# Counting matrices built by TensorE from one-hots of gathered edge runs, with early products in pieces

## The chip, the cores and the metric

The kernel runs on one core of a Trainium2 chip. The metric is the device time of one execution in microseconds. The engines named are PE (TensorE), DVE (VectorE), ACT (ScalarE), POOL (GpSimd) and SP (SyncE, which here only issues transfers). Each engine works through its own instructions in order and waits at semaphores for the others and for DMA.

## The reference, cut to what matters

A graph network on N = 6250 nodes with 128 features, and E = 106250 edges sorted by destination. Four layers, each with a residual and a layer norm:

```python
x = layernorm(x + sage2(x))    # agg = segment_sum(h[src], dst) / max(deg, 1); agg @ Wl + bl + h @ Wr
                               # twice, with a relu between
x = layernorm(x + gcn64(x))    # (x @ W), norm = dinv[src] * dinv[dst], segment_sum, 128 -> 64 -> 128
x = layernorm(x + gcn2(x))     # two such sums
x = layernorm(x + tag(x))      # three inner layers of three hops:
                               # x = segment_sum(w[:, None] * x[src], dst), w = dinv[src] * edge_weight * dinv[dst]
```

So there are two sums over edges in the first layer, one in the second, two in the third and nine in the last. The first five use the number of edges between two nodes; the nine hops use edge weights.

## The kernel before

**Sums as matrix products.** Nodes are cut into 49 windows of 128. Window s of the sources and a chunk of destination windows make a block of a matrix, 128 sources by up to 512 destinations; an entry of `counts` (one byte) says how many edges go from this source to this destination, an entry of `weights` (f32) their summed weight. The destinations are in 13 chunks: eight of 4 windows, three of 3, two of 4. A sum for a chunk runs over its 49 blocks: `counted_sum` (L479) loads seven blocks of bytes at a time (`columns`, L459 and L462, issued by SP), casts two blocks at a time to f32r (L501, on ACT, or on ACT and DVE by turns), and PE multiplies each block by the source table's high and low half (L508), accumulating in PSUM.

**How the matrices are made.** A setup reads the edges and writes per edge its key (destination and source in one number) to DRAM (`keys`), and rows of 17 edges (`recs`). `counts` and `weights` are zeroed by large DMAs (`empty`). Edges are taken as 49 groups of 128 rows of 17 edges. `cell` (from L660) computes on DVE, for each edge of one group, its address in the matrix (`celli`), how often its key recurs among the 48 following edges (the count, `cval`), and, for the 35 groups that concern the first chunks (`dense`), the summed weight (`wval`). `scatter` (L588) then lets POOL write 128 cells per indirect DMA, 17 DMAs for a group: 833 for the counts, 595 for the weights. POOL's indirect DMAs stand in one line (`in_line`), in the order in which they are written down; the count scatters come first, and the weight scatters follow, spread over the products of later stages by `Paced`.

**The stages.** The first sum (to 1209 us) goes chunk by chunk: fetch the edge groups of the chunk after next, zero another chunk, prepare and scatter the groups of the next chunk, degrees of this chunk (17 one-hots per group at L731 and as many matmuls at L732, `norms`), then the 49 blocks of the first sum. As the second sum's table grows with each finished chunk, the loop also makes a part of the second sum's products: `also` uses the same blocks while they are there (sources of earlier chunks, into `half`), and from the eighth chunk on `early_parts` loads blocks of earlier chunks again, two chunks per turn, 144 blocks in all. The rest of the second sum, 190 blocks, follows (to 1311 us), then the sum of the second layer (to 1533), the two sums of the third layer (tile `cols`, two buffers, to 2180), in which small gathers (`gathered_edges`: tiles `gm`, `ge`) bring rows of edges for the hops, standing in POOL's line behind the weight scatters; DVE unpacks them at L882 to L896. The nine hops, which load `weights` (L1245) and gather rows for the remaining destinations, last to the end.

The loads of the first sum use the seven parts of one large room in turn (`slots`).

Of the kernel before, what the change touches and what calls it, by code (L numbers as in the profile page):

```python
# [47 lines left out]
P = 128  # L48
# [39 lines left out]

SLOTS, LOADS, STEP, HOTS, GROUP = 30, 12, 2, 5, 4
# [18 lines left out]
def width(c):  # L108
    return len(windows_of(c)) * P
# [27 lines left out]
def load_weights(nc, a, const, work, ps, ident, tags):  # L137
# [18 lines left out]
    transposed("w1l", a["L0_gnn_W1l"])  # L156
    transposed("w1r", a["L0_gnn_W1r"])
    transposed("w2l", a["L0_gnn_W2l"])
    transposed("w2r", a["L0_gnn_W2r"])
    bcast("b1l", a["L0_gnn_b1l"], D)  # L160
    bcast("b2l", a["L0_gnn_b2l"], D)
# [22 lines left out]
def kernel(ctx: ExitStack, tc: tile.TileContext, a: dict, out: bass.AP):  # L184
# [15 lines left out]
    counts = dram.tile([BASE[NC] + 4 * NB * KD * P, 1], U8, name="counts")  # L200
# [6 lines left out]
    def empty(mats, dt, c, engine):  # L207
        n = 7 * width(c) // (4 if dt == U8 else 16)
        z = zeros[:].bitcast(dt)[:, :n]
        ins = fills[dt, c] = engine.dma_start(  # L210
            mats[BASE[c]:BASE[c + 1]].rearrange("(p s f) o -> p s (f o)", p=P, f=n),
            z.unsqueeze(1).to_broadcast([P, NW * width(c) // n, n])).ins
        tc.declare_no_dep(ins, group=f"cells {dt}", reason="another chunk")
        tc.add_to_no_dep_group(f"cells {dt}", ins)
        return ins

    with tc.tile_pool(name="setup", bufs=1) as setup, \
            tc.tile_pool(name="ps_setup", bufs=2, space=PSUM) as ps:

        def spread(name, ap, dt):  # L220
            t = setup.tile([P, L + 2 * J], dt, name=name)
            nc.sync.dma_start(t[:], bass.AP(ap.tensor, ap.offset, [[L, P], [1, L + 2 * J]]))
            return t
# [4 lines left out]
        dsti = spread("dsti", a["dst"], I32)  # L228
# [3 lines left out]
        main = slice(J, J + L)  # L232


# [3 lines left out]
        nc.vector.tensor_scalar(k1[:], dsti[:], 1023, 13, op0=ALU.bitwise_and, op1=ALU.logical_shift_left)  # L238
        nc.vector.tensor_scalar(k2[:], dsti[:], 20, 23, op0=ALU.logical_shift_right, op1=ALU.logical_shift_left)
# [5 lines left out]
        nc.sync.dma_start(keys[J:].rearrange("(p e) o -> p (e o)", p=P), key[:, main])  # L245


        def field(at):
# [18 lines left out]
        empty(counts, U8, 0, nc.sync)  # L267

# [7 lines left out]
        dst = setup.tile([P, L + 2 * J], F32, name="dst")  # L276
# [6 lines left out]
        nc.vector.tensor_sub(t1[:], dst[:, 2 * J:2 * J + L], dst[:, main])  # L283
        nc.vector.tensor_scalar(t2[:], dst[:, main], float(NOWHERE), None, op0=ALU.is_lt)
        nc.vector.scalar_tensor_tensor(t2[:], t1[:], 0.0, t2[:], op0=ALU.is_equal, op1=ALU.mult)
        nc.vector.tensor_reduce(odd[:, 1:2], t2[:], AX.X, ALU.max)
        nc.vector.tensor_scalar(t2[:], t1[:], float(NOWHERE // 2), None, op0=ALU.is_lt)
        nc.vector.scalar_tensor_tensor(t2[:], t1[:], 1024.0, t2[:], op0=ALU.is_ge, op1=ALU.mult)
        nc.vector.tensor_reduce(odd[:, 2:3], t2[:], AX.X, ALU.max)
# [3 lines left out]
        dmax = setup.tile([P, RPP], F32, name="dmax")  # L293
        nc.vector.tensor_reduce(dmin[:], by_row(dst[:, main]), AX.X, ALU.min)
        nc.vector.tensor_reduce(dmax[:], by_row(dst[:, main]), AX.X, ALU.max)
        rowi = setup.tile([P, RPP], I32, name="rowi")
        nc.gpsimd.iota(rowi[:], pattern=[[1, RPP]], base=0, channel_multiplier=RPP)
        nc.vector.tensor_scalar(rowi[:], rowi[:], ~(P - 1), None, op0=ALU.bitwise_and)
        even = setup.tile([P, RPP], F32, name="even")
        nc.vector.tensor_copy(even[:], rowi[:])  # L300
        d1 = setup.tile([P, RPP], F32, name="d1")
        d2 = setup.tile([P, RPP], F32, name="d2")
        nc.vector.tensor_sub(d1[:], dmax[:], even[:])
        nc.vector.tensor_scalar(d1[:], d1[:], float(2 * P), None, op0=ALU.is_ge)
# [3 lines left out]
        nc.vector.tensor_sub(d2[:], dmin[:], even[:])  # L308
        nc.vector.tensor_scalar(d2[:], d2[:], -float(P), None, op0=ALU.is_lt)
# [6 lines left out]
        row = setup.tile([P, RPP], F32, name="row")  # L316
        nc.gpsimd.iota(row[:], pattern=[[1, RPP]], base=1, channel_multiplier=RPP,
                       allow_small_or_imprecise_dtypes=True)
# [43 lines left out]
    with tc.If(go == 1) as fork:  # L362
        usual_way(tc, a, out, dram, ident, part, first, over, keys, recs, edges, counts, weights, fills, empty)
# [5 lines left out]
def usual_way(ctx, tc, a, out, dram, ident, part, first, over, keys, recs, edges, counts, weights, fills, empty):  # L369
# [9 lines left out]
    iota = const.tile([P, NEAR * P], F16, name="iota")  # L379
    nc.gpsimd.iota(iota[:], pattern=[[1, NEAR * P]], base=0, channel_multiplier=0,  # L380
# [12 lines left out]
    stacked = early.tile([P, DH], F32, name="stacked")  # L393
    nc.vector.tensor_add(stacked[:], ident[:, :DH], ident[:, DH:])
    wt = load_weights(nc, a, early, work, ps, ident, ("y", "pp"))
# [63 lines left out]
    def columns(t, c, mat, dt, step, s0, ws=None):  # L459
        cw, s1 = width(c), min(s0 + step, NW)  # L460
        if ws is None:
            load = nc.sync.dma_start(t[:, :(s1 - s0) * cw], mat[BASE[c]:BASE[c + 1]].rearrange(  # L462
                "(p f) o -> p (f o)", p=P)[:, s0 * cw:s1 * cw]).ins
        else:
            n = len(ws) * P
            load = nc.sync.dma_start(
                t[:, :(s1 - s0) * n].rearrange("p (s f) -> p s f", f=n),
                mat[BASE[c]:BASE[c + 1]].rearrange("(p s f) o -> p s (f o)", p=P, f=cw)[:, s0:s1, :n]).ins
        needs = [ins for i in blocks_of(ws or windows_of(c)) for ins in scattered[dt, i]]
        tc.declare_no_dep(load, group=f"cells {dt}", keep=needs, reason="others' cells")  # L470
        tc.add_to_no_dep_group(f"cells {dt}", load)
        for ins in needs:
            tc.add_manual_dep(load, ins.name, SYNC, reason="the matrix is complete")
        return t
# [4 lines left out]
    def counted_sum(pool, c, parts, turns, own=False, wide_bufs=3, slots=None, since=0, until=NW, also=None):  # L479
# [5 lines left out]
        for s in range(since, until):  # L485
            r = (s - since) % step
            if r == 0:
                t = next(slots) if slots is not None else pool.tile([P, step * CW], U8, name="cols", tag="cols")
                t = columns(t, c, counts, U8, min(step, until - s), s)
                if own:  # L490
                    for j, w in enumerate(windows_of(c)):
                        if s <= w < min(s + step, until):
                            loop = t[:, (w - s) * cw + j * P:(w - s) * cw + (j + 1) * P]
                            nc.vector.tensor_tensor(loop, loop, ident8[:], op=ALU.add)
            if not todo:
# [5 lines left out]
                copy(wide[:, :n * cw], t[:, r * cw:(r + n) * cw])  # L501
                todo = [wide[:, i * cw:(i + 1) * cw] for i in range(n)]
            cols = todo.pop(0)
            for into, of_block, begin, end in [(acc, parts, since, until)] + ([also] if also else []):
                if s < end:
                    lhss = of_block(s)
                    for i, lhs in enumerate(lhss):
                        product = nc.tensor.matmul(into[:, :cw], lhs, cols, start=s == begin and i == 0,  # L508
                                                   stop=s == end - 1 and i == len(lhss) - 1).ins
                paced.product(product, len(lhss))  # L510
# [16 lines left out]
    kept = ctx.enter_context(tc.tile_pool(name="kept", bufs=1))  # L527
# [18 lines left out]
    KNOWN, AHEAD = START[ND], 8  # L546
    halves = {c: dram.tile([P, width(c)], F32, name=f"half{c}") for c in range(1, NC)}
    early_parts = {c: dram.tile([P, width(c)], F32, name=f"early{c}") for c in range(AHEAD)}
# [32 lines left out]
    def scatter(mat, dt, vals, i):  # L581

        group = f"cells {dt}"
        needs = [fills[dt, c] for c in chunks_near(i) if (dt, c) in fills]
        mine = scattered[dt, i] = []
        bounds = {} if dt == U8 else {"bounds_check": mat.shape[0] - 1, "oob_is_err": False}
        for k in range(KD):
            ins = nc.gpsimd.indirect_dma_start(  # L588
                out=mat[:], out_offset=bass.IndirectOffsetOnAxis(ap=celli[:, i, k:k + 1], axis=0),
                in_=vals[:, i, k:k + 1], in_offset=None, **bounds).ins  # L590
            tc.declare_no_dep(ins, group=group, keep=needs, reason="no cell is written twice")
            tc.add_to_no_dep_group(group, ins)
            for need in needs:
                tc.add_manual_dep(ins, need.name, SYNC, reason="empty")
            if dt == F32:
                tc.add_manual_dep(ins, last_count.name, ORDER, reason="needed later")
            mine.append(in_line(ins))
            yield ins
        queue.append(mine[-1])

    class Paced:

        PRODUCTS, GROUP, FIRST = 3.4, 8, 80

        def __init__(self, todo):
            self.todo, self.products, self.begun = todo, 0, 0
            self.some(self.FIRST)

        def some(self, n, behind=None):
            for i in range(n):  # L610
                ins = next(self.todo, None) if self.todo else None
                if ins is not None and i == 0 and behind is not None:
                    tc.add_manual_dep(ins, behind.name, SYNC, reason="the products go ahead")

        def product(self, ins, n):
            self.products += n
# [1001 lines left out]
```

## Time and profile before

| | |
|---|---|
| Time, median of 3 runs | 5791.16 us (5787.49 to 5791.88) |
| Profiled execution | 5791.37 us |
| Its span | 5789.5 us |
| Mean granted TensorE clock | 0.969 |
| PE busy | 5254.7 us (91%) |
| POOL busy | 4158.4 us (72%) |
| DVE busy | 3115.3 us (54%) |
| ACT busy | 2141.4 us (37%) |

The stages, from the table of stretches of the trace (length, busy time of PE, PEld, DVE, ACT and POOL with the number of instructions, granted clock, DMA share, GB/s):

```profile
0.00:33.60 33.60, 1.04 (x3) 0.63 (x3) 27.38 (x53) 7.87 (x7) 1.38 (x11) 1.00 0.69 242
33.60:163.00 129.40, 1.84 (x4) 0.73 (x4) 75.85 (x271) 8.11 (x19) 91.60 (x93) 1.00 0.51 151
163.00:1209.00 1046.00, 757.18 (x3534) 525.63 (x3535) 552.83 (x2123) 439.45 (x586) 800.30 (x807) 0.86 0.63 193
1311.00:1533.00 222.00, 205.03 (x988) 156.37 (x987) 202.54 (x536) 166.36 (x249) 179.73 (x139) 0.98 0.62 179
1533.00:2180.00 647.00, 619.04 (x2925) 512.13 (x2924) 394.31 (x897) 314.79 (x436) 391.57 (x356) 0.99 0.48 137
2180.00:5789.50 3609.50, 3572.44 (x11538) 1868.49 (x11538) 1787.68 (x4748) 1156.77 (x3062) 2614.12 (x2727) 0.99 0.93 316
```

A stage is read by comparing the busy times with its length: the engine whose time comes near to the length bounds it. DMA-issuing work isn't counted as busy on SP, and POOL's busy time here is its indirect DMAs being issued. PEld is the loading of weights for PE and runs beside it. Busy time is less than the time a queue is taken where an engine pauses between instructions, which the groups list as idle time "<-issue".

### The profile page before, as it was taken

To read this page: it belongs to the slowest core of one execution; us is meant where nothing else is said; L and a number is where in the kernel's file an instruction comes from. 1 tells how busy PE (TensorE), PEld (TensorE's weight loads), DVE (VectorE), ACT (ScalarE), POOL (GpSimd) and SP (SyncE) were. 2 spreads that over 40 slices of the span, in tenths; PEclk is the share of its full clock that TensorE was granted. 3 is DMA by queue.
4 is the path that set the end of the run, shared out by engine and by line. 5 is a ranking of instruction groups with operands and counts; after the bars stand their busy time and mean duration, and the time that the engine had idled before them with its cause. 6 is when DMAs were issued, how large, how long until landed. Compare 5 with 4: busy or idle time off the path is not lost.

```text
span 5789.5 us, 70572 instructions
## 1 busy us (share of the span) xinstructions
PE 5254.7 (91%) x19487; PEld 3143.9 (54%) x19487; DVE 3115.3 (54%) x8828; ACT 2141.4 (37%) x4433; POOL 4158.4 (72%) x4204
## 2 busy tenths in 40 slices
PE   0656579799999899999999999999999999999998
PEld 0334457576788784555555555555555555555455
DVE  7685455258855564444446554444456544444566
ACT  1323346347755442323333323323333333233332
POOL 5777777778877617767767767767777677777775
PEclk9878789899999999999999999999999999999999
DMA  5768785146544449999999999999999999999997
GB/s 184 237 201 248 217 260 154 59 140 177 155 131 137 129 139 333 323 319 325 324 318 310 309 313 323 322 321 323 323 302 312 301 326 324 316 323 324 304 336 264
DMA packets 707889, 1517.46 MB, mean 262 GB/s; under 512 B 153094, under 2 KB 359962, under 8 KB 707226
## 3 DMA queue, kind: packets, MB, share of 16 engines
q1 hardware_dynamic: 524642, 1272.39, 65.1%
q0 software_dynamic: 134080, 180.02, 11.5%
q10 hardware_dynamic: 48760, 60.45, 3.1%
q8 instruction: 155, 2.54, 0.2%
q14 instruction: 252, 2.06, 0.1%
HBM read 1313.22 MB, written 199.20 MB: 261 GB/s over the span
## 4 chain that ended last, share of the span: by engine, by line
PE 71%; DMA 11%; POOL 7%; DVE 6%; issue 4%; ACT 1%; ACTq 0%; SPq 0%; POOLq 0%; DVEq 0%
PE acc L1245 45%; PE acc L508 14%; DMA rows<-stored,gsrc 7%; PE gacc L1212 5%; POOL counts L588 5%; PE pp L435 3%; PE pd L732 1%; DMA cols<-counts 1%; POOL weights L588 1%; PE half L508 1%; DMA slots<-counts 1%; DVE widev L501 1%; DMA counts<-cval,celli 1%; ACT wides L501 1%; POOL rows L1148 1%
## 5 line engine op out<-in xcount | busy, mean ns | idle before, releaser
L1245 PE MATMUL acc<-weighed,hop 128*128 128x512 f32 (+1 forms) x7154 | 3402.6, 591 | 13.2 <-DMA weighed<-weights 6.8
L1148 POOL DMA_INDIRECT rows<-stored,gsrc x2727 | 2614.1, 959 | 981.9 <-issue 347.5
L1195 ACT ACTIVATE both<-rows,gwgt 128x128 fp32r<-128x128 f32 x2718 | 1047.8, 400 | 1969.7 <-DMA rows<-stored,gsrc 1783.5
L1212 PE MATMUL gacc<-both,oh 128*128 128x256 f32 x2718 | 1761.2, 657 | 7.9 <-DVE both L1196 7.9
L1245 PEld LDWEIGHTS acc<-weighed,hop 128*128 128x128 f32 x7154 | 1169.7, 190 | 941.2 <-issue 837.6
L1196 DVE SCALAR_TENSOR_TENSOR both<-rows,gwgt,both 128x128 fp32r<-128x128 f32 x2718 | 923.8, 350 | 1334.1 <-ACT both L1195 1323.6
L508 PE MATMUL acc<-wides,t 128*128 128x512 f32 (+1 forms) x3083 | 875.7, 394 | 359.2 <-ACT wides L501 240.3
L588 POOL DMA_INDIRECT counts<-cval,celli x833 | 828.6, 995 | 263.0 <-issue 245.1
L1212 PEld LDWEIGHTS gacc<-both,oh 128*128 128x128 f32 x2718 | 514.6, 190 | 651.8 <-issue 396.2
L508 PEld LDWEIGHTS acc<-wides,t 128*128 128x128 f32 x3083 | 569.8, 191 | 496.9 <-ACT wides L501 267.1
L588 POOL DMA_INDIRECT weights<-wval,celli x595 | 677.2, 1138 | 181.4 <-issue 167.1
L501 ACT CAST wides<-slots 128x1024 fp32r<-128x1024 uint8 (+3 forms) x684 | 562.3, 862 | 521.5 <-DMA slots<-counts 309.2
L508 PE MATMUL acc<-widev,t 128*128 128x512 f32 (+1 forms) x2044 | 576.8, 390 | 31.5 <-DVE widev L501 27.0
L1175 DVE TENSOR_TENSOR oh<-places,gdst 128x640 fp32r<-128x640 f32 x604 | 473.3, 784 | 213.1 <-PE gacc L1212 212.2
L508 PEld LDWEIGHTS acc<-widev,t 128*128 128x128 f32 x2044 | 376.8, 190 | 112.9 <-DVE widev L501 42.8
L731 DVE TENSOR_SCALAR oh<-iota,dloc 128x384 bf16<-128x384 f16 x833 | 214.2, 320 | 366.8 <-PE pd L732 366.7
L501 ACT CAST wides<-cols 128x1024 fp32r<-128x1024 uint8 (+1 forms) x364 | 285.0, 797 | 298.5 <-DMA cols<-counts 160.7
L501 DVE CAST widev<-cols 128x1024 fp32r<-128x1024 uint8 (+1 forms) x364 | 249.8, 691 | 175.2 <-PE acc L508 137.5
L508 PE MATMUL half<-wides,t 128*128 128x512 f32 (+1 forms) x606 | 188.6, 390 | 0.0
L732 PE MATMUL pd<-oh,lw 128*4 128x384 bf16 x833 | 175.4, 334 | 10.1 <-DVE oh L731 8.1
L501 DVE CAST widev<-slots 128x1024 fp32r<-128x1024 uint8 (+3 forms) x239 | 155.8, 669 | 18.2 <-PE acc L508 13.0
L1065 DVE TENSOR_TENSOR y<-pp,dinvw 128x256 f32<-128x256 f32 (+2 forms) x153 | 82.4, 539 | 139.0 <-PE pp L435 138.7
(266 smaller groups left out, 2790.4 us busy)
## 6 DMA issues: line engine op xcount, KB each, us to landing
weighed<-weights SPq DMA_DIRECT2D x1728, 512.0 KB
weights<-zeros SPq DMA_DIRECT2D x8, 12544.0 KB
slots<-counts SPq DMA_DIRECT2D x174, 448.0 KB
cols<-counts SPq DMA_DIRECT2D x140, 448.0 KB
rows<-stored,gsrc POOLq DMA_INDIRECT x2727
counts<-zeros SPq DMA_DIRECT2D x10, 3136.0 KB
weighed<-weights SPq DMA_DIRECT2D x96, 256.0 KB
stored<-hop ACTq DMA_DIRECT2D x74, 256.0 KB
```

Source lines behind the costliest of these rows:

```text
L435: nc.tensor.matmul(pm[:, j * d:(j + 1) * d], xt[:, j * P:(j + 1) * P], w, start=True, stop=True)
L501: copy(wide[:, :n * cw], t[:, r * cw:(r + n) * cw])
L508: product = nc.tensor.matmul(into[:, :cw], lhs, cols, start=s == begin and i == 0, stop=s == end - 1 and i == len(lhss) - 1).ins
L588: ins = nc.gpsimd.indirect_dma_start(out=mat[:], out_offset=bass.IndirectOffsetOnAxis(ap=celli[:, i, k:k + 1], axis=0), in_=vals[:, i, k:k ...
L731: nc.vector.tensor_scalar(oh[:], iota[:], dloc[:, k:k + 1], None, op0=ALU.is_equal)
L732: nc.tensor.matmul(acc[:], lw[:, k, :], oh[:], start=k == 0, stop=k == KD - 1)
L1148: nc.gpsimd.indirect_dma_start(out=fetched_rows[:, self.slot(self.asked), :], out_offset=None, in_=stored[self.h % 2][:], in_offset=bass.I ...
L1175: nc.vector.tensor_tensor(oh[:, :m, :], places[:].unsqueeze(1).to_broadcast([P, m, P]), gdst[:, i, ks].unsqueeze(2).to_broadcast([P, m, P] ...
L1195: nc.scalar.activation(both[:, :D], x, AF.Copy, scale=w)
L1196: nc.vector.scalar_tensor_tensor(both[:, D:], x, w, both[:, :D].bitcast(F32), op0=ALU.mult, op1=ALU.subtract)
L1212: nc.tensor.matmul(self.acc[:, j * 2 * D:(j + 1) * 2 * D], oh, both, start=k == 0, stop=k == KG - 1)
L1245: nc.tensor.matmul(acc[:, :cw], tables[h][:, s, :], t[:, s % STEP * cw:(s % STEP + 1) * cw], start=s == 0, stop=s == NW - 1)
```

## The change

**Counts.** `counts` is one DRAM tile per chunk now, laid out window by window, and no longer zeroed or scattered to. The setup also writes `runs`, 128 keys and 128 weights from each row of 17 edges on, and `begin`, the row from which the edges of four neighbouring nodes are sure to be found. POOL gathers one run for every four nodes (128 runs, that is four windows, in one indirect DMA; 13 of them). `prepared` splits the keys of a batch into zone (source window and which of the four nodes) and place (source within its window), transposes them, and takes the degrees from the same run. For 8 groups of four nodes `hot` makes a zone one-hot (8 x 196) and a place one-hot (8 x 128) on DVE; one matmul per group multiplies them, which gives the counts of four destinations from all sources, and ACT writes two groups at a time as bytes into the window's tile `built`, in runs of eight bytes. SP stores a finished window. Loads read a chunk's seven blocks as one run of 896 bytes per window and partition; casts read them across the windows.

**Pace.** `Meanwhile` is called after every block and does a share of a generator: of the building, 64 evictions in 49 blocks, 81 having been done before the first; and of the zero fills of `weights`, cut into 63 pieces of 1.84 MB, all of which SP issues.

**Weights.** The cells of three edge groups and their 51 scatters come behind each chunk of the first sum, in POOL's one line with the gathers of the runs. The pacing of the weight scatters over later stages is gone.

**Early products.** They begin with the fourth chunk and come in pieces of seven blocks, five pieces a turn (two in the last but one), always for the chunk with most to do: 294 blocks in place of 144, so that 40 remain. The room for loads has five parts, the wide tiles of the first sum two buffers for three, and most of the weights are loaded after the first sum.

```diff
+    def building():
+        found, spots = {}, {}
+        found[0] = gathered_run(0)
+        for w in range(NW):
+            b, c = w // WPB, chunk_of(w)
+            if w % WPB == 0:
+                if b + 1 < NBATCH:
+                    found[b + 1] = gathered_run(b + 1)
+                spots[b] = prepared(b, found.pop(b))
+            t = spare if w % 2 else cells.tile([P, NW * P], U8, name="built")[:]
+            by_column = t.rearrange("p (s f) -> p s f", f=P)
+            for some in range(GROUPS_W // SOME):
+                k0 = w % WPB * GROUPS_W + some * SOME
+                zone = hot("zone", zones2, spots[b], k0, NZ)
+                place = hot("place", places2, spots[b], P + k0, P)
+                for pair in range(SOME // 2):
+                    acc = ps_build.tile([P, 2, CW // 2], F32, name="some")
+                    for i in range(2):
+                        nc.tensor.matmul(acc[:, i, :NZ], place[:, pair, :, i], zone[:, pair, :, i],
+                                         start=True, stop=True)
+                    f = some * SOME * G + pair * 2 * G
+                    nc.scalar.copy(by_column[:, :, f:f + 2 * G].rearrange("p s (i d) -> p s i d", d=G),
+                                   acc[:, :, :NZ].rearrange("p i (s d) -> p s i d", d=G))
+                    yield
+            nc.sync.dma_start(counts[c].rearrange("(w p f) o -> w p (f o)", w=SHAPE[c], p=P)[w - START[c]], t)
+    def hot(name, places, spots, k0, n):
+        t = hots.tile([P, SOME // 2, n, 2], BF16, name=name)
+        nc.vector.tensor_tensor(
+            t[:], places[:].unsqueeze(1).to_broadcast([P, SOME // 2, n, 2]),
+            spots[:, k0:k0 + SOME].rearrange("p (j o) -> p j o", o=2).unsqueeze(2).to_broadcast(
+                [P, SOME // 2, n, 2]), op=ALU.is_equal)
+        return t
+    def gathered_run(b):
+        t = cells.tile([P, 2 * RUN], F32, name="run", bufs=3)
+        ins = nc.gpsimd.indirect_dma_start(
+            out=t[:], out_offset=None, in_=runs[:],
+            in_offset=bass.IndirectOffsetOnAxis(ap=begin[:, b:b + 1], axis=0)).ins
+        queue.append(in_line(ins))
+        return t
...
+    meanwhile = Meanwhile()
+    meanwhile.add(building(), 4 * PAIRS_W / NW)
+    meanwhile.some(0, 5 * PAIRS_W + 1)
...
+    meanwhile.add(filling, (ND + 1) * FILLS / (NW * 11))
...
     for c in range(NC):
-            fetch_chunk(c + 2)
-            if c + 4 < NC:
-                empty(counts, U8, c + 4, nc.sync)
-            count_cells(c + 1)
-            for i in sorted(i for i in blocks_near(c) if i in degs):
-                degrees(i)
-            norms(c)
...
-            for e in range(2 * (c - ND + 1), 2 * (c - ND + 2)):
-                if 0 <= e < AHEAD:
-                    half = fetched_sums(halves[e]) if e > 0 else None
-                    acc = counted_sum(counted, e, both(t1hi, t1lo), [(2, "s")], slots=slots,
-                                      since=START[e], until=KNOWN)
+            for e, since, m in pieces.get(c, ()):
+                half = fetched_sums(partial[e]) if e in partial else None
+                acc = counted_sum(counted, e, both(t1hi, t1lo), [(2, "s")], wide_bufs=2, slots=slots,
+                                  since=since, until=since + m, meanwhile=meanwhile)
...
+            for i in dense[PER * c:PER * (c + 1)]:
+                filled(chunks_near(i))
+                cell(i, fetch(i))
+        meanwhile.rest()
-    last_count = queue[-1]
-    paced = Paced(ins for i in dense for ins in scatter(weights, F32, wval, i))
...
-                copy(wide[:, :n * cw], t[:, r * cw:(r + n) * cw])
+                copy(wide[:, :n * cw].rearrange("p (s w f) -> p s w f", s=n, f=P),
+                     t[:, :, r:r + n, :].rearrange("p w s f -> p s w f"))
```

## The prediction

> **What bounds the kernel now.** I read the stretches of the span first, then the groups, then the waits up to 1209 us, where the last product of the first sum ends.
>
> ```profile
> 300.00:400.00 100.00, 68.75 (x314) 39.67 (x315) 74.34 (x286) 31.57 (x44) 77.44 (x75) 0.85 0.72 222
> 1000.00:1100.00 100.00, 72.45 (x376) 57.32 (x375) 26.00 (x106) 40.13 (x58) 76.23 (x79) 0.86 0.18 55
> 1209.00:1311.00 102.00, 98.10 (x500) 79.96 (x499) 74.70 (x204) 48.02 (x76) 79.66 (x73) 0.95 0.58 168
> 1430.00:1530.00 100.00, 93.75 (x466) 73.14 (x466) 95.47 (x247) 80.72 (x126) 81.92 (x60) 1.00 0.66 187
> 1600.00:1700.00 100.00, 99.41 (x440) 79.61 (x439) 56.53 (x95) 51.63 (x67) 78.06 (x73) 1.00 0.47 135
> 2500.00:2600.00 100.00, 99.35 (x311) 50.47 (x310) 38.22 (x94) 26.53 (x71) 60.53 (x64) 1.00 0.93 314
> ```
>
> The columns are length, busy us of PE, PEld, DVE, ACT and POOL, the granted clock, the DMA share and GB/s. Until 1209 no engine is full: PE has 50 to 95 us in 100 and POOL stands at 76 throughout. That is an issuing queue: 79 scatters in 100 us, 1.27 us each. From 1209 (rest of the second sum) to 2180 PE is the bound, except in the next layer's sum (1311 to 1533), where DVE has 95. The hops from 2180 on are full on PE and DMA; the diff leaves them alone.
>
> ```profile
> L588 POOL DMA_INDIRECT counts<-cval,celli x833 | 828.6, 995 | 263.0 <-issue 245.1
> L588 POOL DMA_INDIRECT weights<-wval,celli x595 | 677.2, 1138 | 181.4 <-issue 167.1
> L501 ACT CAST wides<-slots 128x1024 fp32r<-128x1024 uint8 (+3 forms) x684 | 562.3, 862 | 521.5 <-DMA slots<-counts 309.2
> L508 PE MATMUL acc<-widev,t 128*128 128x512 f32 (+1 forms) x2044 | 576.8, 390 | 31.5 <-DVE widev L501 27.0
> L731 DVE TENSOR_SCALAR oh<-iota,dloc 128x384 bf16<-128x384 f16 x833 | 214.2, 320 | 366.8 <-PE pd L732 366.7
> ```
>
> The count scatters, 833 x 1.27 = 1058 us, pace the first sum: its loads of counts wait for them, which the waits show (total us, times, longest).
>
> ```profile
> ACT wides L501 <- DMA slots<-counts: 309.2, 11, 90.8
> PE acc L508 <- DMA slots<-counts: 123.1, 2, 118.7
> ```
>
> **The change, by steps.** Base: the profiled execution, 5791.37 us (span 5789.5 and 1.9 around it); the three runs have a median of 5791.16, the same thing.
>
> *Removed:* 833 count scatters, the counts' zero fills, and 833 one-hots and matmuls for degrees. *Added on DVE:* 196 zone and 196 place one-hots (1568 and 1024 bf16) and 13 preparations of a gathered run; *on PE* 1568 matmuls of 196 columns; *on ACT* 784 evictions of 392 elements; *on SP* 49 stores of 802 KB. One zone with its place is a "hot" and makes 4 evictions. Hots are spread so that one falls to 3.06 blocks (81 evictions go ahead, then 64 in 49 blocks).
>
> ACT per hot: the PSUM copy of 384 columns takes 0.477, so 0.483 for 392, x4 = 1.93, and casts of 3.06 blocks at 1.045 a pair 1.60: 3.5 us. An eviction writes bytes in runs of 8; the nearest strided row is the edge copy with 4-byte elements 12 bytes apart (L270, 850 elements 1.354 against 0.907 for L264): ends 0.48 and 0.70; I take 0.48, since 8 bytes lie together. In "SBUF — State Buffer", Specifications, the Trainium skill asks for two hits per 16-byte line; eight-byte runs would meet that, the edge copy, one or two per line, would not, and its row agrees; by the rule the sum stays, by the row it gains 784 x 0.22, at most 172 us on ACT.
>
> DVE per hot: 2592 elements. Two-operand rows run at one element a tick (816 elements 0.995, 512 0.685, so 1.02 ns each): 2.8 us. The only row with all operands 16 bits wide, L731, takes 0.257 us for 384 back to back, 0.67 ns each: 1.7 us; I take 1.7, since that row is nearest in type, and keep 2.8. The rule in "VectorE: DVE Perf Modes", Mode 2x_1P, gives a two-tensor operation two elements per cycle where all are 16-bit with unit step; the 816-element rows have f32 inputs and can't show it; by the rule a hot is about 1.5 and the sum stays, by the f32 rows it is rival (b), 100 us more. Besides hots, a chunk carries 3 cell preparations (about 7 us each: four operations of 816 elements and some 17 of 0.17), one run's preparation (about 7) and the stage's work (about 8): 36 us. Over 16 hots (chunks 0 to 2) that makes 3.95 a hot, over 27 (chunks 3 to 7, with early pieces) 3.0, less than ACT's 3.5.
>
> PE per hot: 8 matmuls between 0.094 (half of L732's 384 columns, 0.184) and 0.184, and 3.06 blocks of two or four products at 0.234: 2.3 to 4.4; I take 2.9 in most segments.
>
> So without further waits: first products at about 118 us (163 now): 64 evictions of 0.5 from about 70, then a store and a load of about 12; chunks 0 to 2 at 16 x 3.95 + 11 = 74 each (11 being the turn of a chunk: L563 waits up to 11.0 us); chunks 3 to 7 at 27.4 x 3.55 + 11 = 108; chunks 8 to 12, the build over, 290 together (for chunk 8: 162 products of 384 columns at 0.175, 70 of 512 at 0.234, turn 11). 118 + 222 + 540 + 290 = 1170, 39 less than now.
>
> *After the first sum.* 40 blocks remain of 190: 40 x 2 x 0.234 = 19 on PE, and about 6 us of stage work per chunk now rules: 77 for 102, so -25. POOL's weight scatters have then been done, and with them goes this stall near 1991:
>
> ```profile
> 1985.85 0.24 DVE L882 TENSOR_SCALAR gdst<-gm 128x17 f32<-128x17 f32 x1 [11.42 <-DMA gm<-recs,gat]
> ...
> 1991.78 2.07 PE L508 MATMUL acc<-widev,t 128*128 128x512 f32 x4 [14.68 <-DVE widev L501]
> ```
>
> The gathers stood behind POOL's scatters, DVE stood in them, and PE lost 15: -16 with its tail. Counts are loaded in 896-byte runs for 3584 and cast from a strided view. I cost both at nothing from 1311 on: DMA share 0.47 to 0.66 covers the loads; if 20% slower (262 GB/s at share 0.95 while fills ran, 868 to 903, against 314 in the hops), loads of 3.5 us pass the 3.3 in which PE uses one, and 140 of them lose up to 0.6 each, 84. If the DVE cast of 1024 (0.69) falls to one element a tick (1.1), the 239 of the sum at 95% lose about 100.
>
> *What is moved, and the step that decides.* The 595 weight scatters move into the first sum, 51 behind each chunk's three cells. POOL issues in order, and the gathers of the runs stand in the same line: in the changed order of POOL, the gathers for batches 4, 5, 6, 7, 9, 10 and 12 each come directly behind 51 scatters: 51 x 1.27 = 65 us, 69 with the landing. In DVE's order the preparation that waits for the gather comes only 8 to 12 hots after the first of these cells' indices (from hot 29 to 41, 49 to 57, 64 to 73, 92 to 100, 112 to 120, 134 to 143, 158 to 167). At 3.5 to 4 us that is 28 to 48 us: DVE arrives first and waits. Behind the waiting preparation stand all later hots, hence matmuls, evictions, SP's store and the count loads behind the store. As a cycle: 69 us from a cell to its preparation, then the hots to the next cell at 3.5 to 3.9: 100 + 96 + 141 + 112 + 118 + 122 + 176 = 865 us from hot 29 (13 behind the 16 sent ahead, about 150) to the last (1015). Add 20 to the end of chunk 7 and 290: 1325, 116 later than 1209. The weights' fills (63 of 1.84 MB on SP, two to four pressed in front of the first chunks' cells) could hold a scatter for the 7 us that one takes at 262 GB/s; within the range.
>
> Sum: 5791 + 116 - 25 - 16 = 5866 us.
>
> **Rivals.** (a) *The gathers are in time:* DVE arrives later than I count, or POOL issues faster without count work. For it: 36 us of DVE per chunk may fall between cell and preparation; against: the positions in order. Then 1170 stands: 5791 - 39 - 25 - 16 = 5711, faster. It decides once the first sum ends by 1250 (1209 + 25 + 16), that is, once the seven waits cost it under 80 us, 11 each. (b) *Hots at one element a tick:* 2.8 for 1.7. The cycle then has 104 hots outside its waits at about 4.3 for 3.7, 62, and the 29 before it are 1.1 longer each, 32: with chunk ends about +100, 5966. For it: every two-operand row; against: none of those has 16-bit inputs. (c) *Eviction at 0.70, or slow casts or loads later on:* ACT to 4.4 a hot adds 50 to 80; casts or loads up to 100: 5920 to 5965. (d) *The transfers fill up:* fills, stores and loads of chunks 3 to 7, some 32 MB in 108 us, 296 GB/s, against 262 to 314 seen at full share; if they set the pace with neither waits nor gains, 5780 to 5800.
>
> **How the numbers follow.** Forecast 5866 with its own range 5820 to 5910: chance 0.45; (a) 0.17; (b) 0.13; (c) 0.17; (d) 0.08. (a) reaches down to 5711 with part-waits above it, so the range starts at 5730 and leaves about one in ten out below; above, 5985 takes in (b) and (c) one at a time and leaves both at once out. A measurement can tell 0.2% here, 11.6 us. Faster: (a) and a third of (d), 0.20; same: 0.05; slower: 0.75.
>
> **What would show it.** DVE waiting for the DMA of a run, seven times of 20 to 40 us, before 1020, with POOL in scatters of weights meanwhile: right. No such wait and a first sum ending near 1170: rival (a). A zone one-hot of 1.6 us rather than about 1.05: (b). An eviction mean over 0.6, a DVE cast over 0.9: (c). DMA share over 0.9 with loads as the longest wait: (d). PE's 15 us gap before the last sum's end should be gone and the hops last 3608 as now; if the hops change, the sum is wrong in a place I did not look.

## The result, and the profile after

The changed kernel takes 5842.4 us (median of 4 runs, 5837.23 to 5845.64) against 5790.8 for the kernel before: 1.0089 times as long, 95% interval 1.0072 to 1.0107. Its profiled execution took 5844.81 us, span 5842.9, clock 0.967. The forecast was 5866, and the mechanism that it called likeliest was the right one.

Stages are told by the same events in both traces: the last product with `w2r` ends the first sum, the last with `wconv` the rest of the second, the last with `wlin` the second layer's sum, the first with `weighed` the third layer. The prediction's 1209, 1311 and 1533 us were read from other events, so only differences of lengths are held against it.

| stage ends at, us (length) | before | after | difference of lengths |
|---|---|---|---|
| first sum | 1214.7 | 1318.2 | +103.5 |
| rest of the second sum | 1357.5 (142.8) | 1450.8 (132.6) | -10.2 |
| second layer | 1543.5 (186.0) | 1632.3 (181.5) | -4.5 |
| third layer | 2173.5 (630.0) | 2227.4 (595.1) | -34.9 |
| hops, last such product | 5773.9 (3600.4) | 5827.5 (3600.1) | -0.3 |

The sum of the differences is 53.6 us; the profiled executions differ by 53.4.

The waits of the changed kernel up to 1400 us (total us, times, longest):

```profile
DVE ki L778 <- DMA run<-runs,begin: 298.2, 8, 46.4
PEld L866 <- DVE place L830: 255.2, 19, 45.0
PE some L866 <- DVE place L830: 248.7, 14, 44.7
POOL weights L648 <- DVE low L755: 182.5, 4, 64.4
```

DVE waits for gathered runs, and PE behind it for the next one-hots. Of the eight waits for runs one, of 4.9 us, is for the very first run. Now DVE's timeline, the first instruction of each preparation (start, duration; in brackets the wait before it):

```profile
172.82 0.21 DVE L778 CAST ki<-run 128x128 int32<-128x128 f32 x1
229.56 0.23 DVE L778 CAST ki<-run 128x128 int32<-128x128 f32 x1 [35.82 <-DMA run<-runs,begin]
334.75 0.23 DVE L778 CAST ki<-run 128x128 int32<-128x128 f32 x1 [40.70 <-DMA run<-runs,begin]
434.07 0.23 DVE L778 CAST ki<-run 128x128 int32<-128x128 f32 x1 [39.46 <-DMA run<-runs,begin]
572.70 0.23 DVE L778 CAST ki<-run 128x128 int32<-128x128 f32 x1 [46.35 <-DMA run<-runs,begin]
575.96 0.22 DVE L778 CAST ki<-run 128x128 int32<-128x128 f32 x1
686.97 0.23 DVE L778 CAST ki<-run 128x128 int32<-128x128 f32 x1 [43.23 <-DMA run<-runs,begin]
814.35 0.23 DVE L778 CAST ki<-run 128x128 int32<-128x128 f32 x1 [44.59 <-DMA run<-runs,begin]
816.25 0.22 DVE L778 CAST ki<-run 128x128 int32<-128x128 f32 x1
943.94 0.23 DVE L778 CAST ki<-run 128x128 int32<-128x128 f32 x1 [43.15 <-DMA run<-runs,begin]
```

Seven waits of 36 to 46 us stand before batches 4, 5, 6, 7, 9, 10 and 12, while 8 and 11, whose gathers were issued right behind the ones before, have none. POOL's timeline gives the other half of the first one: a scatter of the first cells at 152.02, the gather behind the 51 of them at 226.76. The other bursts of 51 in front of a gather take as long, 71.6 to 75.1 us from the first scatter to the gather.

```profile
152.02 1.03 POOL L648 DMA_INDIRECT weights<-wval,celli  x1 [86.63 <-DVE celli L756]
...
226.76 0.99 POOL L766 DMA_INDIRECT run<-runs,begin  x1 [0.30 <-issue]
```

In the stretches of 200 us no engine of the changed kernel is full in the first sum (the columns are as before):

```profile
118.00:318.00 200.00, 125.24 (x659) 81.28 (x657) 120.50 (x259) 125.61 (x236) 107.72 (x93) 0.84 0.74 224
318.00:518.00 200.00, 125.46 (x679) 80.79 (x680) 117.97 (x242) 127.85 (x241) 90.14 (x76) 0.83 0.67 209
518.00:718.00 200.00, 106.27 (x562) 68.44 (x561) 87.15 (x183) 103.93 (x194) 98.77 (x94) 0.77 0.60 182
```

The later stages, in the same columns (the end of the first sum, then about the second layer, the third and the hops), are as full as they were:

```profile
1030.00:1318.00 288.00, 249.85 (x1209) 198.46 (x1208) 88.96 (x255) 176.36 (x241) 221.56 (x213) 0.98 0.43 117
1401.00:1625.00 224.00, 203.84 (x975) 156.35 (x975) 199.29 (x538) 165.01 (x250) 0.00 (x0) 0.97 0.61 167
1625.00:2233.00 608.00, 597.44 (x2913) 507.90 (x2912) 377.64 (x890) 318.04 (x433) 33.07 (x30) 1.00 0.52 145
2233.00:5842.90 3609.90, 3569.32 (x11542) 1864.93 (x11541) 1793.27 (x4748) 1162.00 (x3062) 2616.02 (x2727) 0.99 0.93 317
```

And the groups that answer to those of before:

```profile
L648 POOL DMA_INDIRECT weights<-wval,celli x595 | 670.9, 1128 | 565.3 <-DVE low L755 182.5
L544 ACT CAST wides<-slots 128x1024 fp32r<-128x1024 uint8 (+3 forms) x703 | 611.8, 885 | 226.0 <-PE half L552 83.5
L552 PE MATMUL acc<-widev,t 128*128 128x512 f32 (+1 forms) x1964 | 538.8, 386 | 24.9 <-DVE agg L564 12.7
```

The count scatters are gone, and with them the 309 us in which ACT waited for counts; from 1401 us on POOL issues nothing until the next small gathers for the hops. In the first sum, up to 718 us, PE, DVE and ACT are each busy 44 to 64% of the time, and the transfers are at 0.60 to 0.74: a picture of engines that wait for one another in turn.

### The profile page after: what moved, and what is told of

Same layout as the page of the kernel before. It is cut to its first block, busy times and chain, and to the rows that moved or that the text cites. A ratio compares the mean times of both kernels' runs of the same rounds, so it can differ in the third digit from the quotient of the medians.

```text
span 5842.9 us, 70969 instructions
## 1 busy us (share of the span) xinstructions
PE 5292.9 (91%) x20205; PEld 3176.3 (54%) x20205; DVE 3119.8 (53%) x7885; ACT 2464.2 (42%) x5187; POOL 3345.4 (57%) x3393
## 5 line engine op out<-in xcount | busy, mean ns | idle before, releaser
L552 PE MATMUL acc<-wides,t 128*128 128x512 f32 (+1 forms) x3163 | 993.9, 409 | 77.6 <-ACT wides L544 69.5
L544 ACT CAST wides<-slots 128x1024 fp32r<-128x1024 uint8 (+3 forms) x703 | 611.8, 885 | 226.0 <-PE half L552 83.5
L552 PE MATMUL acc<-widev,t 128*128 128x512 f32 (+1 forms) x1964 | 538.8, 386 | 24.9 <-DVE agg L564 12.7
L866 PE MATMUL some<-zone,place 128*128 128x196 bf16 x1568 | 265.4, 267 | 271.2 <-DVE place L830 248.7
L1004 POOL DMA_INDIRECT gm<-recs,gat x17 | 18.0, 1059 | 849.3 <-DVE gwgt L1021 846.7
L544 ACT CAST wides<-cols 128x512 fp32r<-128x512 uint8 (+1 forms) x364 | 289.1, 798 | 238.2 <-PE acc L552 182.2
L866 PEld LDWEIGHTS <-place 128*128 128x128 bf16 x1568 | 118.8, 103 | 419.1 <-DVE place L830 255.2
L869 ACT CAST slots<-some 128x392 uint8<-128x392 f32 x384 | 177.1, 513 | 151.7 <-PE some L866 143.2
L869 ACT CAST built<-some 128x392 uint8<-128x392 f32 x400 | 184.6, 516 | 133.5 <-PE some L866 130.1
L830 DVE TENSOR_TENSOR zone<-zones,spots 128x1568 bf16<-128x1568 bf16 x196 | 189.9, 969 | 73.8 <-PE some L866 73.3
```

The source lines that it names most:

```text
L544: copy(wide[:, :n * cw].rearrange("p (s w f) -> p s w f", s=n, f=P), t[:, :, r:r + n, :].rearrange("p w s f -> p s w f"))
L830: nc.vector.tensor_tensor(t[:], places[:].unsqueeze(1).to_broadcast([P, SOME // 2, n, 2]), spots[:, k0:k0 + SOME].rearrange("p (j o) -> p ...
L866: nc.tensor.matmul(acc[:, i, :NZ], place[:, pair, :, i], zone[:, pair, :, i], start=True, stop=True)
L869: nc.scalar.copy(by_column[:, :, f:f + 2 * G].rearrange("p s (i d) -> p s i d", d=G), acc[:, :, :NZ].rearrange("p i (s d) -> p s i d", d=G))
```

## The experiments

**Gathers asked for earlier.**

```diff
-            t = cells.tile([P, 2 * RUN], F32, name="run", bufs=3)
+            t = cells.tile([P, 2 * RUN], F32, name="run", bufs=6)
-            found[0] = gathered_run(0)
+            found.update((b, gathered_run(b)) for b in range(4))
-                    if b + 1 < NBATCH:
-                        found[b + 1] = gathered_run(b + 1)
+                    if b + 4 < NBATCH:
+                        found[b + 4] = gathered_run(b + 4)
```

> Edit: the gathers of the runs are asked for four batches ahead instead of one (six run buffers for three); nothing else moves. Theory (the line on POOL decides): DVE's wait for the runs, 298.2 us in 8 times in the changed kernel, falls under 30, POOL's scatters stay at 595, and the first sum ends at about 1180 instead of 1318 (the no-wait sum of the prediction was 1170); time about 5705. Rival (the waits hide work that would set the pace anyway, ACT at 3.5 us a hot, the turns of the chunks, transfers): the waits go but the first sum ends at 1250 or later, time 5775 or more.

**Weights scattered later.** `scatter` becomes a generator again and is paced by `Paced`, as in the kernel before.

```diff
             nc.vector.tensor_add(wval[:, i, :], w, f1[:])
-            scatter(i)
...
         meanwhile.rest()
+    paced = Paced(ins for i in dense for ins in scatter(i))
```

> Edit: the cells are still prepared in the first sum, but the 595 scatters of weights are issued after it, paced over later products as before the change; the gathers of the runs stay one batch ahead. Theory (the line): without scatters in front of them the gathers come in time, the first sum ends near 1180 as with gathers asked for earlier. The later stages get back what the scatters cost there: the gap of 15 us on PE near the end of the third layer and, if the rest of that layer's 35 us less came from POOL's scatters too, all 35: about 5740. Rival for the 35 (the new layout of the counts or its loads brought 20 of them): only 15 return, about 5720. Rival for the first sum (other work sets the pace): 5790 or more.

**Early products as before the change.**

```diff
-        for c in PIECES:
-            known, pieces[c] = START[c + 1], []
...
+        for c in range(ND - 1, NC):
+            for e in range(2 * (c - ND + 1), 2 * (c - ND + 2)):
+                if e < ND:
+                    pieces.setdefault(c, []).append((e, START[e], START[ND] - START[e]))
+                    done[e] = START[ND]
```

> Edit: the second sum's early products as before the change (144 blocks, two chunks a turn from the eighth chunk on), everything else as changed, so 192 blocks remain instead of 126. Theory (POOL's line sets the pace of a chunk, 51 scatters each): without pieces a chunk of the build has 16 hots and still 69 us of scatters in front of the next gather, so the waits grow in number, to 10 or more and over 350 us; the first sum gets longer, about 1390, and the rest of the second sum 10 longer: about 5920. Rival (pieces only add products to the first sum): it gets 66 x 2 x 0.234 = 31 us shorter, time about 5825.

These three fell on a chip where the kernel before took 7821.74 us. They gave 6899.82, 6808.57 and 6924.71 there; none of the expectations in microseconds can be held against that. Their traces did show the mechanism: no wait for a run, but for the first of about 5 us, with gathers asked for earlier or weights scattered later, and 296.0 us of them in 9 times with the early products of before. All three were run again, beside a fourth, on a chip where the kernel before takes 5801.74.

> The kernel of e1_runs_ahead again (runs asked for four batches ahead, scatters of weights where the change put them), because its first runs fell on a chip where the kernel before took 7821.74 us instead of 5791. Theory (POOL's line): no wait of DVE for a run; with the build then bound at about 3.57 us a hot, as the weights-late kernel showed from 75 to 775 us, the first sum ends between 1050 and 1120; time 5600 to 5680. Rival (the scatters themselves, sharing the transfers with fills, stores and loads, hold the loads back): the waits for runs go but loads of counts take their place; first sum at 1200 or later, 5730 or more.

Measured: 5588.08 us (5580.08 to 5591.78), ratio to the kernel before 0.9631 (0.9615 to 0.9647). The first sum ends at 1055.2 instead of 1318.2. DVE's timeline has no wait at the same instructions, except the very first of 4.89 us. Four of the thirteen:

```profile
197.20 0.32 DVE L778 CAST ki<-run 128x128 int32<-128x128 f32 x1
258.35 0.32 DVE L778 CAST ki<-run 128x128 int32<-128x128 f32 x1
326.01 0.22 DVE L778 CAST ki<-run 128x128 int32<-128x128 f32 x1
404.65 0.21 DVE L778 CAST ki<-run 128x128 int32<-128x128 f32 x1
```

And the stretches show what the waits had held back, on every engine:

```profile
118.00:318.00 200.00, 170.47 (x909) 109.92 (x908) 169.45 (x367) 171.77 (x323) 135.64 (x101) 0.96 0.95 293
318.00:518.00 200.00, 175.52 (x975) 112.23 (x973) 150.87 (x313) 179.78 (x339) 161.15 (x128) 0.98 1.02 313
518.00:718.00 200.00, 166.95 (x889) 109.83 (x887) 147.05 (x308) 159.93 (x300) 160.46 (x130) 0.94 0.95 284
```

The same 595 scatters are still issued beside the first sum, from 151.7 to 1059.6 us. So it was the place of the gathers in POOL's line, not the scatters' work, that made the change slower: moving 13 gathers takes 263 us out of the first sum. The rival's sign is missing too: between 118 and 790 us ACT waits only 5.6 us for loads of counts.

> The kernel of e2_weights_late again (scatters of weights after the first sum, paced over later products). Theory: first sum at about 1040 as in its first run, the rest of the third layer back to about 630 from 595, the rest of the second sum and the second layer's sum a little longer with scatters beside them (by up to 15): about 5620. Rival (the scatters' cost comes back in full where they stand now, since POOL still needs 595 x 1.27 = 756 us before the hops' gathers): the hops start late, 5750 or more.

Measured: 5567.93 us (5566.14 to 5574.56), ratio 0.9594 (0.9577 to 0.961). First sum 1038.7, rest of the second 131.3, second layer 185.2, third layer 594.5, hops 3607.2. The rival fell. The first sum and the total were as expected or better, but the return to 630 in the third layer did not come, although POOL is full of scatters there:

```profile
1355.00:1455.00 100.00, 100.00 (x458) 82.81 (x458) 61.50 (x113) 54.73 (x70) 78.78 (x70) 1.00 0.52 139
1455.00:1555.00 100.00, 100.00 (x484) 85.80 (x484) 57.68 (x99) 54.50 (x73) 78.74 (x70) 1.00 0.51 137
```

So scatters beside the products cost PE nothing there. The gap of 15 us near the end of the third layer stays away because POOL's scatters let the small gathers go at 1754.74 us, and DVE comes to them only at 1770.3; in the kernel before DVE stood ready from 1974.4 on and the gathers went at 1983.32. The rest of the third layer's gain has another source, looked for below. No other version measured is faster; the one with both edits, below, equals it.

The trace also shows that the scatters are not all as late as the edit says: 167 of the 595 still go out before 1038.7 us. But only 13 of them stand before the last gather of a run (492.37 us), never more than three between two gathers. What is gone is the burst in front of a gather.

> The kernel of e3_early_as_before again (144 early blocks, two chunks a turn from the eighth on). In its first run DVE waited 296.0 us for runs in 9 times and the first sum ended at 1481. Theory (waits stay, and the work follows the pace of the scatters): first sum 1350 to 1390, time 5890 to 5930. Rival (pieces only add products to the first sum): 5825 or less.

Measured: 5850.13 us (5844.9 to 5851.84), ratio 1.0082 (1.0065 to 1.0099), against 1.0089 for the change. Both expectations missed. The waits grew, 336.5 us in 9 times, but the first sum still got shorter, 1298.7 for 1318.2, and the later stages longer (140.1, 185.1 and 604.6 for 132.6, 181.5 and 595.1). The pieces therefore make no difference to the total that can be measured while the waits stand; beside the faster variants they were not tried.

> Both edits: runs asked for four batches ahead and weights scattered late. Theory: nothing more stands before the gathers in r2, so asking ahead adds nothing: within 10 us of r2. Rival (the gathers' own landing still delays DVE): 20 us or more below r2.

Measured: 5571.6 us (5568.06 to 5574.49), ratio 0.9601 (0.9585 to 0.9617): as expected, the two edits cure one thing.

**What paces the build now.**

> The weights-late kernel with the zero fills of the weights spread over the whole first sum (one in 13.4 blocks instead of one in 8.6, and none forced before a group's cells, since the scatters come later). During the build the weights-late and runs-ahead kernels show the transfers at a share of 0.94 to 1.02 (285 to 325 GB/s) and ACT at 0.8 to 0.9. Theory 1 (with POOL's line out of the way the transfers set the pace of the build): a third of the fills leaves the build, some 40 MB or 130 us of transfers; ACT's 3.5 us a hot then allows 20 to 60 us: the first sum ends at 980 to 1020, time 5510 to 5550. Theory 2 (ACT and PE set it): first sum at 1035, time within 10 of 5568.

Measured: 5575.4 us, ratio 0.9622 (0.9606 to 0.9638), but the run tells nothing apart: SP issued the last of the 63 fills at 703.0 us, against 665.6 in the weights-late kernel, since only the point where they are written down had moved. The first sum ends at 1046.5. A second version orders them behind loads:

```diff
+            if loaded:
+                tc.add_manual_dep(ins, loaded[-1].name, ORDER, reason="its turn")
```

> As v5_fills_spread, but each fill of the weights stands behind the last load of counts of its time in SP's order, because in v5 SP still issued all 63 fills by 718 us. Now some 38 of 63 should be issued by 775. Theory 1 (the transfers set the pace of the build): the first sum ends at 980 to 1020 and the time is 5510 to 5550. Theory 2 (ACT and PE set it, 3.5 us a hot): DMA share falls to about 0.75 in the build and the first sum still ends at 1030 to 1045, time within 10 of 5568.

It ran on a chip where the kernel before takes 7894.08 us (it took 6897.5), so its time can't be used. Until 518 us its trace should be comparable, because the weights-late kernel made 225 one-hots (zones and places) between 118 and 518 on the chip of its second run and 226 on the slow chip of its first, which is not this one. The one-hots by stretch (columns: length, DVE busy and count, clock, DMA share, GB/s), first weights late in its second run:

```profile
118.00:318.00 200.00, 87.65 (x111) 0.99 0.97 306
318.00:518.00 200.00, 90.83 (x114) 0.97 1.00 320
```

then with the fills ordered:

```profile
118.00:318.00 200.00, 92.36 (x118) 1.00 0.86 276
318.00:518.00 200.00, 86.90 (x110) 0.98 0.85 269
```

That is 225 against 228, while the DMA share fell from 0.98 to 0.85. The pace did not follow the transfers; ACT was busy 0.90 of this stretch in the one kernel and 0.92 in the other. That favours theory 2 here. It isn't settled for the whole sum: after 518 us the kernel with ordered fills falls behind (its first sum ends at 1083.4, the weights-late kernel's on the other slow chip at 1044.3), which neither theory named, and what such a version takes where the kernel before takes 5800 stays open.

**Where the third layer's 35 us came from.** In the kernel before, four products of 128x512 take 0.93 us from start to start in the third layer, in the changed one 0.907. A product has two operands: the node table's window is the stationary one, loaded into PE beforehand, and the wide tile, the cast block, is the moving one. Two edits moved tiles of the kernel before by an unused tile of 64 bytes, in front of the node tables in one (shown) and behind them, in the pool `kept`, in the other:

```diff
+    shift = const.tile([P, 16], F32, name="shift")
+    nc.vector.memset(shift[:], 0.0)
```

> The kernel before, with one unused tile of 64 bytes per partition put in front of the node tables, so that every later tile in SBUF lies 64 bytes further on; no other instruction changes except one memset. In the kernel before, a product of 128x512 follows the last after 0.2334 us in every stage; in the changed kernel and all made from it after 0.2269. Theory (where the tables lie in SBUF decides: their start modulo 128 is 32 before and 96 in the changed kernel, and would be 96 here): 0.227, the third layer's two sums 15 us shorter, time about 5775 to 5785 where the kernel before takes 5800. Rival (something else in the changed program): 0.2334 and no difference in time.

Measured: products at 0.2325 us, 5793.45 us against 5795.1, ratio 1.0 (0.999 to 1.0009). The rival held.

> The kernel before with an unused tile of 64 bytes per partition placed behind the node tables, so that the wide tiles (the moving operand) start 64 bytes further on and the tables (the stationary one) stay. In the kernel before and in x1 the two starts differ by 192 modulo 256 bytes and products follow each other after 0.233 us; in the changed kernel by 0, at 0.227; here they differ by 0. Theory (the difference of the two starts decides): 0.227, third layer 15 us shorter, about 5770 to 5785 where the kernel before takes 5795. Rival (another cause in the program): 0.233 and no difference.

> The kernel of x2_wides_shifted again, since it ran on the chip where the kernel before takes 7894 us; there products followed each other after 0.227 us and the time was 0.44% less. Theory (the difference of the two starts, 0 instead of 192 modulo 256, gives 0.227 in all five sums): on a chip where the kernel before takes about 5795, some 5000 products x 0.006 = 30 us less, 5760 to 5775, and the third layer's sums at 610 to 615 instead of 630. Rival (0.227 came from that chip): 0.233 and 5790 to 5800.

Measured: first, on that slow chip, products at 0.225 to 0.230 us and ratio 0.9956 (0.9933 to 0.998); then, in the second run, 0.2275, but 5800.6 us against 5794.62, ratio 1.0007 (0.9997 to 1.0017). The rate was as expected, the time was not. PE's timeline in the third layer, the kernel before:

```profile
1601.58 1.10 PE L508 MATMUL acc<-widev,t 128*128 128x512 f32 x4
1602.51 1.09 PE L508 MATMUL acc<-wides,t 128*128 128x512 f32 x4
```

and with the wide tiles shifted:

```profile
1601.17 1.07 PE L508 MATMUL acc<-widev,t 128*128 128x512 f32 x4
1602.07 1.07 PE L508 MATMUL acc<-wides,t 128*128 128x512 f32 x4
...
2001.76 2.07 PE L508 MATMUL acc<-widev,t 128*128 128x512 f32 x4 [31.41 <-DVE widev L501]
```

Four products take 0.90 to 0.91 us instead of 0.93, and the gap that was 14.68 us is now 31.41. PE comes to this wait 6.8 us earlier (1970.35 for 1977.10). It waits for DVE, DVE for the gathers behind POOL's scatters, and these go when POOL has come to them, here even 10.0 us later (1993.36 for 1983.32). The third layer takes 637.0 us, for 630.0. So POOL's line was a bound of this stage too, and the measured wait was only the part of it that PE's slower products had not covered.

## Why the prediction was right, and where its terms were off

*The deciding step* was right in place, number and cause: the seven batches named are the seven that wait, and a kernel with only the gathers moved loses the waits and is 3.7% faster than the kernel before. The waits were larger than worked out, 293 us in seven where the forecast's own terms (69 us in each of seven, less 63 hots in all at 3.5 to 4 us) give 231 to 263. The term that was off is the scatter: priced at 1.27 us, it took 1.40 to 1.47 in the seven bursts, so that a burst and the landing of its gather last 74 to 78 us. That the fills and stores beside them did this was not tested. Of the 293 us, 263 reached the end of the first sum.

*The first sum's end* was forecast 116 later and came 103.5 later. The cycle from the first scatter to the last eviction of the build measured 898 us (152.0 to 1049.8) for 865. What stood behind it was put too long: 268 us to the end of the sum for 310. These two errors nearly cancel. By an estimate, some 13 of the 42 us are early blocks that the forecast counted for the last chunks and the program's lists (below) don't hold, 28 blocks of 2 x 0.234 us.

*The no-wait sum*, 1170, was the worst number, though only rival (a) rests on it: the kernels without waits end at 1055 and 1039. It adds the turns of a chunk, 11 us for each of eight chunks, 88 in all. In the kernel with earlier gathers the build lasts from 75 to 788 us, 3.64 us for each of 196 hots with everything in it, near the 3.55 priced without turns; so the turns seem to be covered by other hots, though they were not traced one by one. Rival (a), put at 5711, is 5588 when it is made true, and the waits cost 4.6% of the time of the kernel before (1.0089 less 0.9631), some 265 us, not the 155 that 5866 less 5711 gives.

*The rest of the second sum* was put at -25 and came to -10.2. The term rested on a wrong count: the lists that the program makes hold 210 early blocks and leave 126 of 192, not 294 and 40 of 190; a piece is taken only where seven blocks are ready, so the five pieces a turn aren't always found. The description of the change ahead of the prediction has the same error. The count alone doesn't explain the miss, since 126 blocks are 59 us on PE and the term stood at 77 for the stage's other work. PE's busy time in this stage fell by 24 us (136.7 to 112.9), but its idle time rose by 14 (6.1 to 19.7): it now waits 14.8 us, in 6 times, for DVE's `agg` (L564) at the turns of chunks, which it did not before. That much of the work between chunks no longer hides behind products.

*The third layer* was put at -16 and came to -34.9. The 15 us gap went as forecast. By an estimate from the rates, some 13 more came from the product's rate, which nothing in the diff's arithmetic changes: 1960 products of 512 columns at 0.0065 us less, while those of 384 columns hardly change. The shifted runs show that the kernel before could not have used that rate, since POOL's line stood behind. About 7 us stay unexplained.

*The second layer* was put at nothing and got 4.5 us shorter; no run looked into it. The product's rate would make 3 of it (490 products of 512 columns) if PE set the pace, but DVE is about as busy there (169.3 us of 181.5, for PE's 171.1).

*The sum* came out right in part by luck. Against the forecast the first sum is 12.5 us shorter, the rest of the second 14.8 longer, the third layer 18.9 and the second layer 4.5 shorter: errors of up to 19 us that leave 21 in all. The sign and the place of the loss are not luck, as the kernels without the waits show.

*Rivals (b), (c), (d)* fell by their own signs. For (b) and (c) these are in the groups of the changed kernel (count, then shortest, median and longest in ns):

```profile
L830 DVE TENSOR_TENSOR zone<-zones,spots x196: 939/968/1044, 73.7 to 1044.2; 128x1568 bf16<-128x1568 bf16 x196
L830 DVE TENSOR_TENSOR place<-places,spots x196: 657/683/730, 74.7 to 1045.1; 128x1024 bf16<-128x1024 bf16 x196
...
L869 ACT CAST built<-some x400: 463/496/667, 77.5 to 1049.8; 128x392 uint8<-128x392 f32 x134
```

From 1024 to 1568 elements the one-hot of 16-bit operands grows by 0.285 us, 0.52 ns an element, half the 1.02 ns of the rows with f32 inputs. That is the two elements per cycle that "VectorE: DVE Perf Modes", Mode 2x_1P, of the Trainium skill gives for a two-tensor operation on 16-bit types. A hot's pair takes 1.65 us, as priced from L731. The eviction's median is 0.496 us (0.48 was taken, 0.70 the bound) and its mean 0.516. This row agrees with the rule of two hits per 16-byte line in "SBUF — State Buffer", Specifications, which runs of eight bytes meet. The DVE cast of 1024 is still 0.69 through the strided view, against the 0.9 that (c) named. For (d), the DMA share is at most 0.84 in stretches of 200 us up to 918 us, ACT's waits for loads of counts come to 4.2 us between 118 and 1050, and the hops are unchanged to 0.3 us.

## What to carry to other kernels

Where one queue issues in order, look not only at how much work moves onto it but at who stands behind the burst, and compare the burst's length with the distance, in the consumer's own instructions, to the point where it is needed: here 51 scatters, 75 us, against 8 to 12 hots of 3.6 us. Thirteen gathers asked for four batches earlier turned 0.9% slower into 3.7% faster, the scatters later into 4.1%.

A measured wait need not be all that stands behind it: make the engine in front faster, and the wait can grow by what was gained, as the gap of 14.68 us did when it became 31.41.

## What the runs showed of the hardware

- **The granted clock was lower where PE waited.** Between 118 and 718 us it was 0.77 to 0.84 with the waits for runs, and 0.94 to 0.98 without them in the same stretches.
- **A product's rate depends on where its operands lie.** With starts of the moving and the stationary operand apart by 192 modulo 256 bytes (the kernel before, and both shifted together) a 128x512 product follows after 0.2325 to 0.235 us; with a difference of 0 (the changed kernel and all made from it, and the wide tiles shifted alone) after 0.225 to 0.230. Neither start alone decides: the shifted-alone kernel has its tables where the slow kernel before has them, and its wide tiles where the slow kernel with both shifted has them. Only these two differences were tried; why it is so was not shown.
- **Two of the chips were far slower.** On them the kernel before took 7822 and 7894 us and the variants made from the changed kernel 6809 to 6925. The hops took 4506 us for 3600 in the variant with earlier gathers, and its first sum 1443 for 1055; with the weights late the first sum was 1044 for 1039. No trace of the kernel before was taken on either, and the cause stays open.
